# GpSimd takes the last eight rows of the small systems, and the solving of group 6, L1 and the last outputs are issued elsewhere

## The chip, the cores and the metric

The kernel runs on one core of a Trainium2 chip, as one launch of one program. Its engines are TensorE (PE in the profile, with PEld for its weight loads), VectorE (DVE), ScalarE (ACT), GpSimd (POOL) and SyncE (SP, which here only issues transfers). The metric is the device time of the launch in microseconds (us), lower is better. Times are medians of several executions; the profile is of one execution more.

## The reference, cut to what matters

A stream x of 128 sequences with 32 tokens of 128 channels runs through four layers. Each layer adds three blocks to the stream: cross attention, attention, and a feed-forward block.

```python
x = x + L0_xattn(layernorm(x), ctx)     # cross attention over 257 context rows, 16 heads
x = x + L0_attn(layernorm(x))           # kernel attention with landmarks, below
x = x + L0_ffn(layernorm(x))            # 8 experts, the best 2 of each token
x = x + L1_xattn(layernorm(x), ctx, mask); x = x + L1_attn(layernorm(x)); x = x + L1_ffn(layernorm(x))
...                                     # L2 and L3, three blocks each
```

The block around which the change turns is L0's attention. It solves one linear system for each sequence and head:

```python
Phi_Q = exp(-sq_dists(Q, landmarks) / temperature)
Phi_K = exp(-sq_dists(K, landmarks) / temperature)
W_kernel = exp(-sq_dists(landmarks, landmarks) / temperature) + REG * eye(64)
Z = einsum('bhnk,bhnd->bhkd', Phi_K, V)
Y = linalg.solve(W_kernel, Z)
out = einsum('bhnk,bhkd->bhnd', Phi_Q, Y)
norm = einsum('bhnk,bhko->bhno', Phi_Q, linalg.solve(W_kernel, sum(Phi_K, -2)[..., None]))
return (out / maximum(norm, 1e-10)) @ Wo.T + bo
```

L1's three blocks are a depooling cross attention, a state-space block (a convolution over time, a scan, a gate) and 16 experts of which each token uses 4.

## The kernel before, in words

**Groups.** The 4096 tokens are held in SBUF as eight groups (0 to 7) of 512 tokens, tiles `X0` to `X7` of 128 partitions x 4 x 128. A group is 16 sequences.

**Stage 1, L0's cross attention (`L0_xattn`).** A loop over 128 sequences, n = 0 to 127 (and two more turns to drain), 16 for each group. Each turn computes scores (line 544), reductions of their maximum on VectorE (546), exponentials on ScalarE (548), transposes and values on TensorE (566, 569, 583, 584). At the end of each turn `side_steps(3, 8)` advances other work, held in queues of Python generators: three steps of `kq` (the kernels of L0's attention, `L0_attn_kernels`, for the group before), steps of `sq` (the solving, `L0_attn_solve`) until the costs that they yield add up to 8, and one step of `oq` (the outputs, `L0_attn_out`). When the kernels of a group are through they append its solving to `sq`, and the solving appends its outputs to `oq`. So group 6's kernels run in the turns after n = 113, group 6's solving from about n = 120, and group 7's kernels begin when the loop is over.

**The solving (`L0_attn_solve`).** One group has 16 sequences x 16 heads = 256 systems of 32 unknowns (the 64 landmarks are folded onto the 32 tokens) with 9 right-hand sides. 128 partitions hold 2 systems each in a tile `A` of 32 rows x 2 x 41. It is loaded by 32 transfers, 16 of which read what the kernels stored (706) and 16 the right-hand sides (708). The elimination has 32 pivots k: a clamped reciprocal (712, 713), the scaled `row` (716), and then, for each block of eight rows below the pivot, a product into a temporary (722) and a subtraction from `A` (724), all on VectorE; ScalarE copies the row back (726). The matrix is symmetric, so the factors are read from row k itself. The back substitution has 31 products and subtractions (729, 731). The result goes to memory in eight transfers (737), and the outputs load it again for each tile of four sequences (748), multiply it with the other kernel matrix (756) and add the projection to `X` (770).

**Stage 2, L0's experts (`L0_ffn`).** Four chunks, m = 0 to 3, of two groups each. `L0_ffn_front` normalizes, routes, and sorts tokens by expert (`dispatch`, whose compares on VectorE fill tiles `dSL` for TensorE); `L0_ffn_blocks` runs 23 blocks of 128 gathered tokens through one expert's weights each, with gathers of tokens and weights issued by GpSimd; `L0_ffn_back` gathers the results in 16 gathers into tiles `G` and adds them to the stream (1026). TensorE's instructions of this stage stay in the order in which the program issues them: `order()` chains each to the one before. The fronts of chunks 0, 1 and 2 lie beside the kernels of group 7, chunk 0 and chunk 1. Chunk 3 holds groups 6 and 7, so its front needs their outputs.

Between blocks `side(nk, us, no, nl)` advances the queues of stage 1 (with a budget `us` for the solving and `no` steps of the outputs) and `nl` steps of `dq`, which from chunk 1's fourth block on holds L1 for groups 0 and 1, one generator of 28 steps each (2 of cross attention, 6 of the state-space block, 20 of the experts, 16 of which are one expert each). What is left of L1 at the end runs behind chunk 3.

**The rest.** `middle` runs L1 for groups 2 to 7 beside L2's cross attention and attention, then come L2's experts and L3. The change does not touch them. A scheduler places each engine's instructions when the program is built, within the dependencies and the chains above: an engine's queue need not be in the order of the source.

Of the kernel before, what the change touches and what calls it, by code (L numbers as in the profile page):

```python
# [9 lines left out]
FP = mybir.dt.float32  # L10
# [3 lines left out]
ALU = mybir.AluOpType  # L14
# [154 lines left out]
class Kern:  # L169
# [202 lines left out]
    def L0_xattn(self, W):  # L372
        nc = self.nc
        with self.pool("xw") as xw:
# [62 lines left out]
            with self.pool("xc") as xc, self.pool("xs", 2) as xs, \  # L437
# [5 lines left out]
                for n in range(B + 2):  # L443
# [29 lines left out]
                    if i == 3 and b == 1 and g + 1 < NG:  # L473
                        nxt = self.L0_xattn_group(g + 1, WNf, xc)
                    if t:
                        self.side_steps(3, 8)

    def follow(self, st, *insts):

# [213 lines left out]
    def L0_attn_solve(self, g):  # L693
# [16 lines left out]
        for k in range(T):  # L710
            p = sv.tile([128, HC], FP, tag="p", bufs=2)
            nc.vector.tensor_scalar(p, A[:, k, :, k], 1e-6, None, ALU.max)
            nc.vector.reciprocal(p, p)
            n = N - 1 - k
            row = sv.tile([128, HC, N], FP, tag="row", bufs=2)
            nc.vector.tensor_tensor(row[:, :, k + 1:N], A[:, k, :, k + 1:N], p.unsqueeze(2).to_broadcast([128, HC, n]), ALU.mult)
            yield 0.3 + 0.00107 * HC * n
            for i0 in range((k + 1) // RB * RB, T, RB):
                i0, i1 = max(i0, k + 1), i0 + RB
                m, n = i1 - i0, N - i0  # L720
                t = sv.tile([128, RB * HC * N], FP, tag="t", name="elt")[:, :m * HC * n].rearrange("p (i h j) -> p i h j", i=m, h=HC)
                nc.vector.tensor_tensor(t, A[:, k, :, i0:i1].rearrange("p h i -> p i h").unsqueeze(3).to_broadcast([128, m, HC, n]),  # L722
                                        row[:, :, i0:N].unsqueeze(1).to_broadcast([128, m, HC, n]), ALU.mult)
                nc.vector.tensor_tensor(A[:, i0:i1, :, i0:N], A[:, i0:i1, :, i0:N], t, ALU.subtract)  # L724
                yield 0.12 + 0.00214 * m * HC * n
            nc.scalar.copy(A[:, k, :, k + 1:N], row[:, :, k + 1:N])
        for k in range(T - 1, 0, -1):
            t = sv.tile([128, RB * HC * N], FP, tag="t", name="elt")[:, :k * HC * R].rearrange("p (i h j) -> p i h j", i=k, h=HC)
# [48 lines left out]
    def dispatch(self, pool, psum, tag, I8, n, k, E, NB):  # L777
# [63 lines left out]
        yield 1  # L841
        ps = psum.tile([128, NB], FP, tag=tag, name="pinv")
        for i in range(n * k):
            SL = pool.tile([128, 128], FP, tag="dSL", bufs=3)
            nc.vector.tensor_scalar(SL, self.j128, qf[:, i, 0:1], None, ALU.is_equal)
            nc.tensor.matmul(ps, lhsT=SL, rhs=BK[:, i, :], start=i == 0, stop=i == n * k - 1)
            if i % 4 == 3 and i < n * k - 1:
                yield 1
# [8 lines left out]
    def L0_ffn(self, w, W):  # L857
        nc = self.nc
        with self.pool("fs", 2) as fs, self.pool("fr", 2) as fr, \
# [25 lines left out]
            for m, c in enumerate(chunks):  # L885
# [1 line left out]
                if m + 1 < 4 and m < 2:  # L887
                    fr_ = self.L0_ffn_front(m + 1, chunks[m + 1], w, fs, fr, fpb, new)
                for b, _ in enumerate(self.L0_ffn_blocks(cur[0], fs, fpa, fpb)):
                    side(0, 4.0, int(m > 0 and (m < 2 or b > 18)))  # L890
                    if old and b == 3:
                        self.L0_ffn_back(*old, fs)
                        if m == 1:
                            self.dq = [self.L1(g, W) for g in range(2)]
                    if fr_ and b >= 3 and next(fr_, None) is None:
                        fr_ = None
                    order()
                while fr_ and next(fr_, None) is not None:
                    order()
                if m == 2:  # L900
                    while not self.ready.issuperset(chunks[3]):
                        side(1, 6.5, 1)
                        order()
                    for _ in self.L0_ffn_front(3, chunks[3], w, fs, fr, fpb, new):
                        side(0, 0, 0)
                        order()
# [112 lines left out]
    def L0_ffn_back(self, m, c, slot, rows, inv, E2, fs):  # L1019
        nc = self.nc  # L1020
        for i in range(8):
            x = self.X[c[i // 4]][:, i % 4, :]
            for j in range(2):
                G = fs.tile([128, 128], FP, tag="G", bufs=6)
                self.gather(G, self.ysd[m], slot[:, i, j:j + 1])
                nc.vector.scalar_tensor_tensor(x, G, E2[:, i, j:j + 1], x, ALU.mult, ALU.add)

# [907 lines left out]
```

## Time and profile before

| what | us |
|---|---|
| median of 3 runs | 5004.54 |
| lowest and highest run | 5003.34, 5005.09 |
| the profiled execution | 5007.62 |
| its span, first to last instruction | 5005.9 |
| end of L0's cross attention on TensorE | 2113.9 |
| last store of a kernel matrix of group 7 | 2203.4 |
| loads of group 7's systems, first and last issue | 2205.5, 2249.9 |
| solve 6: first pivot, end of back substitution | 2044.0, 2237.9 |
| solve 7: first pivot, end of back substitution | 2274.2, 2423.1 |
| chunk 0, first block and last | 2217.7, 2290.2 |
| chunk 1, first block and last | 2297.0, 2576.0 |
| chunk 2, first block and last | 2583.7, 2716.5 |
| chunk 3, first block and last | 2785.4, 2836.7 |
| last addition of chunk 3 | 2867.5 |

The span runs from the first to the last instruction of the profiled execution; its own time has 1.7 us more. Rows of the profile name a line of the kernel, an engine, an operation and the tiles, output first; a tile's buffer number is left out. A wait is put down to the instruction that released it.

### The profile page before, as it was taken

The page shows a single profiled execution, that of the slowest core. Times are in us where ns is not written, and L with a number is a line of the kernel's source. Part 1 is how long each engine was busy: PE and PEld are TensorE (multiplying, and loading weights), DVE is VectorE, ACT ScalarE, POOL GpSimd, SP SyncE. Part 2 cuts the span into 40 slices and gives each one's busy share as a digit, 9 for nine tenths or more (in the row PEclk, how much of TensorE's full clock was granted, in tenths as well). Part 3 has the DMA queues.
Part 4 walks back from the last instruction along what each step waited for, and adds up shares of the span by engine and source line. Part 5 has one row for each costly group of instructions (what it writes and reads, how often), then busy time and mean ns, then how long its engine had stood idle before and what let it go on. Part 6 is the DMA issues. An engine that isn't in the chain of part 4 may idle for free. (4 is left out here: it accounts for less than half of the span.)

```text
span 5005.9 us, 90275 instructions
## 1 busy us (share of the span) xinstructions
PE 4248.2 (85%) x33802; PEld 3111.7 (62%) x33802; DVE 3387.4 (68%) x10311; ACT 2347.2 (47%) x6637; POOL 1295.6 (26%) x1309
## 2 busy tenths in 40 slices
PE   7999999999898999875377798898898886879788
PEld 5777676767676776665365565666566653546455
DVE  5336758494948576777655478888898775777444
ACT  4555445454444444432233354545554554763333
POOL 1020211111110202035143513332332332322443
PEclk8999899999999998967677898999999987989677
DMA  4223131314141222255132410111011101000100
GB/s 139 61 60 57 39 66 42 66 39 72 38 72 35 56 53 56 49 121 144 37 107 86 138 35 23 31 29 28 27 29 32 37 20 46 1 1 16 32 14 10
DMA packets 388968, 255.95 MB, mean 51 GB/s; under 512 B 184545, under 2 KB 356961, under 8 KB 388017
## 3 DMA queue, kind: packets, MB, share of 16 engines
q1 hardware_dynamic: 361842, 191.22, 16.1%
q0 software_dynamic: 18240, 58.66, 4.0%
q8 instruction: 266, 4.36, 0.4%
q10 hardware_dynamic: 8448, 0.30, 0.2%
q14 instruction: 172, 1.41, 0.1%
HBM read 211.02 MB, written 39.08 MB: 50 GB/s over the span
## 5 line engine op out<-in xcount | busy, mean ns | idle before, releaser
L218 POOL TENSOR_TENSOR rs<-ve,w_const 128x4 f32<-128x4 f32 (+1 forms) x192 | 189.9, 990 | 1552.1 <-DVE ve L216 1278.4
L544 PE MATMUL S<-cT,q 128*128 128x257 f32 x2048 | 545.5, 407 | 18.5 <-ACT E L548 17.8
L544 PEld LDWEIGHTS S<-cT,q 128*128 128x128 f32 x2048 | 391.0, 201 | 145.7 <-issue 54.6
L546 DVE TENSOR_REDUCE nm<-S 128x1 f32<-128x257 f32 x512 | 214.8, 420 | 335.9 <-PE S L544 334.6
L1389 PE MATMUL S<-cT,QM 128*128 128x289 f32 x1024 | 326.4, 435 | 78.5 <-ACT E L1391 70.5
L548 ACT ACTIVATE E<-S,nm 128x257 f32<-128x257 f32 x512 | 242.3, 474 | 299.8 <-DVE nm L547 298.8
L1391 ACT ACTIVATE E<-S,nm 128x289 f32<-128x289 f32 x512 | 253.4, 499 | 194.8 <-DVE nm L1390 190.9
L722 DVE TENSOR_TENSOR elt<-A,row 128x400 f32<-128x400 f32 (+22 forms) x608 | 290.0, 477 | 6.4
L724 DVE TENSOR_TENSOR A<-A,elt 128x400 f32<-128x400 f32 (+22 forms) x608 | 291.2, 479 | 4.2
L527 PE MATMUL pq<-xT,WQK 128*128 128x128 f32 x2048 | 268.0, 290 | 14.1 <-ACT q L528 14.1
L1389 PEld LDWEIGHTS S<-cT,QM 128*128 128x128 f32 x1024 | 177.5, 198 | 161.8 <-ACT E L1391 72.3
L583 PE MATMUL po<-TA,cN 128*128 128x512 f32 x512 | 271.1, 612 | 4.7 <-DVE xn L224 3.9
L527 PEld LDWEIGHTS pq<-xT,WQK 128*128 128x128 f32 x2048 | 252.5, 200 | 24.7 <-ACT q L528 17.6
L584 PE MATMUL po<-TB,cN 128*128 128x512 f32 x512 | 265.5, 600 | 0.0
L558 ACT ACTIVATE E<-E,sm 128x256 f32<-128x256 f32 x512 | 220.2, 498 | 79.8 <-DVE sm L554 74.9
L241 POOL TENSOR_TENSOR QM<-QT,w_const 128x512 f32<-128x512 f32 x128 | 142.6, 1119 | 434.0 <-PE S L1389 410.7
L1390 DVE TENSOR_REDUCE nm<-S 128x1 f32<-128x289 f32 x512 | 219.8, 449 | 31.1 <-PE S L1389 28.3
L1400 PE MATMUL pt<-w_const,E 128*96 128x128 f32 (+1 forms) x1536 | 234.9, 290 | 0.0
L597 PE MATMUL pout<-WVO,OT 128*128 128x128 f32 x2048 | 234.2, 276 | 0.3 <-ACT OT L585 0.3
L597 PEld LDWEIGHTS pout<-WVO,OT 128*128 128x128 f32 x2048 | 231.7, 192 | 0.9 <-ACT OT L585 0.5
L1400 PEld LDWEIGHTS pt<-w_const,E 128*96 128x96 f32 (+1 forms) x1536 | 181.5, 145 | 61.6 <-issue 37.3
L1721 ACT ACTIVATE E<-S,nm 128x128 f32<-128x128 f32 x512 | 179.9, 397 | 64.6 <-DVE nm L1718 64.6
(526 smaller groups left out, 10357.3 us busy)
## 6 DMA issues: line engine op xcount, KB each, us to landing
cT<-ctxT SPq DMA_DIRECT2D x128, 257.0 KB
cN<-ctx SPq DMA_DIRECT2D x128, 256.0 KB
cT<-ctxT SPq DMA_DIRECT2D x32, 514.0 KB
phik<-PW SPq DMA_DIRECT2D x32, 256.0 KB
phiq<-P SPq DMA_DIRECT2D x32, 256.0 KB
A<-phik SPq DMA_DIRECT2D x128, 64.0 KB
PQ<-phiq SPq DMA_DIRECT2D x32, 256.0 KB
cN<-ctx SPq DMA_DIRECT2D x32, 194.0 KB
```

Source lines behind the costliest of these rows:

```text
L527: self.follow(st, nc.tensor.matmul(ps[:, k, :, :], lhsT=WQK[:, 4 * j + k, cb * 128:(cb + 1) * 128], rhs=t["x"], start=True, stop=True))
L544: self.follow(st, nc.tensor.matmul(S, lhsT=t["QP"][j][:, cb, b, :, :], rhs=t["cT"][b][:, cb, :], start=cb == 0, stop=cb == 1))
L548: nc.scalar.activation(E[:, j, 0:LK], S, AF.Exp, bias=m, accum_out=sm[:, j:j + 1])
L558: nc.scalar.activation(E[:, j, 0:256], E[:, j, 0:256], AF.Copy, scale=sm[:, j:j + 1])
L583: self.follow(st, nc.tensor.matmul(po, lhsT=cN[:, 0, c], rhs=TA, start=True, stop=False), nc.tensor.matmul(po, lhsT=cN[:, 1, c], rhs=TB, s ...
L584: nc.tensor.matmul(po, lhsT=cN[:, 1, c], rhs=TB, start=False, stop=True))
L597: self.follow(st, nc.tensor.matmul(po[:, 0, :], lhsT=OT[:, cb, h, :, :], rhs=WVO[:, cb, h, :], start=h == 0 and cb == 0, stop=False))
L722: nc.vector.tensor_tensor(t, A[:, k, :, i0:i1].rearrange("p h i -> p i h").unsqueeze(3).to_broadcast([128, m, HC, n]), row[:, :, i0:N].uns ...
L724: nc.vector.tensor_tensor(A[:, i0:i1, :, i0:N], A[:, i0:i1, :, i0:N], t, ALU.subtract)
L1389: self.follow(st, nc.tensor.matmul(S, lhsT=t["QM"][:, 0, 4 * j:4 * j + 4, :], rhs=t["cT"][:, b, :], start=True, stop=True))
L1391: nc.scalar.activation(E[:, j, :], S, AF.Exp, bias=nm[:, j:j + 1], accum_out=sm[:, j, b:b + 1])
L1400: self.follow(st, nc.tensor.transpose(pt[0:n, j * 128:(j + 1) * 128], E[:, j, k0:k1], self.ident))
```

## The change

Edits in the order of work, one of engine, and sizes of buffers:

- the turns of stage 1 from n = 120 on have a budget of 0 for the solving;
- in `L0_attn_solve`, for all groups but the last, the product and the subtraction for rows 24 to 31 are issued on GpSimd, with a temporary of their own (`tp`); such an update yields 0.01 in place of its cost; `row` has three buffers in place of two;
- in `L0_ffn` the budget of each block is 3.0 in place of 4.0; outputs are stepped only in chunk 1; L1 is stepped in every second block from chunk 1 on;
- behind chunk 2, L1 and the solving are stepped together until no solving is left and L1 of group 0 is through, then six steps of L1 alone, then the outputs, one for one with steps of L1, until chunk 3's groups are complete;
- `dSL` has two buffers in place of three, `G` three in place of six.

```diff
@@ L0_xattn
-                        self.side_steps(3, 8)
+                        self.side_steps(3, 8 if n < 120 else 0)
@@ L0_attn_solve
-            row = sv.tile([128, HC, N], FP, tag="row", bufs=2)
+            row = sv.tile([128, HC, N], FP, tag="row", bufs=3)
...
-                nc.vector.tensor_tensor(t, A[:, k, :, i0:i1].rearrange("p h i -> p i h").unsqueeze(3).to_broadcast([128, m, HC, n]),
-                                        row[:, :, i0:N].unsqueeze(1).to_broadcast([128, m, HC, n]), ALU.mult)
-                nc.vector.tensor_tensor(A[:, i0:i1, :, i0:N], A[:, i0:i1, :, i0:N], t, ALU.subtract)
-                yield 0.12 + 0.00214 * m * HC * n
+                eng = nc.vector
+                if g < NG - 1 and i0 == T - RB:
+                    eng = nc.gpsimd
+                    t = sv.tile([128, RB * HC * (RB + R)], FP, tag="tp", name="eltp").rearrange("p (i h j) -> p i h j", i=m, h=HC)
+                eng.tensor_tensor(t, A[:, k, :, i0:i1].rearrange("p h i -> p i h").unsqueeze(3).to_broadcast([128, m, HC, n]),
+                                  row[:, :, i0:N].unsqueeze(1).to_broadcast([128, m, HC, n]), ALU.mult)
+                eng.tensor_tensor(A[:, i0:i1, :, i0:N], A[:, i0:i1, :, i0:N], t, ALU.subtract)
+                yield 0.12 + 0.00214 * m * HC * n if eng is nc.vector else 0.01
@@ dispatch
-            SL = pool.tile([128, 128], FP, tag="dSL", bufs=3)
+            SL = pool.tile([128, 128], FP, tag="dSL", bufs=2)
@@ L0_ffn
-                    side(0, 4.0, int(m > 0 and (m < 2 or b > 18)))
+                    side(0, 3.0, int(m == 1), int(m < 1 or b % 2))
...
                 if m == 2:
+                    while self.sq or len(self.dq) > 1:
+                        side(0, 4.0, 0)
+                        order()
+                    for _ in range(6):
+                        side(0, 0, 0)
+                        order()
                     while not self.ready.issuperset(chunks[3]):
-                        side(1, 6.5, 1)
+                        side(0, 0, 1)
                         order()
@@ L0_ffn_back
-                G = fs.tile([128, 128], FP, tag="G", bufs=6)
+                G = fs.tile([128, 128], FP, tag="G", bufs=3)
```

## The prediction

> **What bounds the kernel now.** I read the page's sums, then the stages, then the waits of TensorE in the stage with most idle time, then single rows.
>
> The page says that no engine is full:
>
> ```profile
> span 5005.9 us, 90275 instructions
> ...
> PE 4248.2 (85%) x33802; PEld 3111.7 (62%) x33802; DVE 3387.4 (68%) x10311; ACT 2347.2 (47%) x6637; POOL 1295.6 (26%) x1309
> ```
>
> So I cut the span at events: the end of the cross attention (2114), of the last kernels (2204), solve 7 from its first pivot to its last back substitution (2274 to 2423), the first block of expert chunk 2 (2584), its last (2717), the first of chunk 3 (2785), its last (2840). Columns are the stretch, its length, and the busy time of each engine.
>
> ```profile
> core 0: us, PE busy (x) PEld busy (x) DVE busy (x) ACT busy (x) POOL busy (x), PEclk, DMA share, GB/s
> 1876.00:2114.00 238.00, 218.65 (x1940) 162.81 (x1939) 157.95 (x510) 115.62 (x306) 40.57 (x43) 0.93 0.22 46
> ...
> 2274.00:2423.00 149.00, 52.02 (x387) 47.45 (x387) 123.34 (x389) 29.40 (x100) 55.91 (x49) 0.63 0.28 85
> ...
> 2584.00:2717.00 133.00, 91.44 (x540) 73.70 (x540) 58.64 (x173) 52.06 (x126) 57.17 (x58) 0.82 0.36 102
> 2717.00:2785.00 68.00, 53.16 (x262) 39.63 (x260) 52.47 (x179) 13.70 (x26) 31.62 (x32) 0.77 0.21 65
> 2785.00:2840.00 55.00, 50.92 (x417) 46.44 (x419) 10.75 (x25) 37.93 (x112) 32.54 (x34) 1.00 0.68 215
> 2840.00:2876.00 36.00, 9.26 (x39) 5.59 (x32) 19.69 (x53) 6.50 (x8) 20.91 (x21) 0.58 0.30 88
> ```
>
> Cross attention is TensorE's (92% in the first row). Solve 7 is VectorE's, with TensorE at 35%. The waits of TensorE between 2340 and 2460 name the hole:
>
> ```profile
> engine line waited for: us in total, times, longest us
> PE ko L756 <- DVE Yb L690: 76.1, 1, 76.1
> ```
>
> TensorE's queue is in program order in this layer; the outputs of group 7 (L756) stand between blocks 5 and 6 of chunk 1, and need solve 7. From there 17 blocks, all of L1 for groups 0 and 1, and chunks 2 and 3 follow in 430 us.
>
> **The rows on GpSimd.** For groups 0 to 6 the updates of rows 24 to 31 move: 24 pivots x 2 instructions x 7 groups = 336. On VectorE they are these rows:
>
> ```profile
> L724 DVE TENSOR_TENSOR A<-A,elt 128x272 f32<-128x272 f32 x192 | 84.0, 437 | 0.2
> L722 DVE TENSOR_TENSOR elt<-A,row 128x272 f32<-128x272 f32 x192 | 83.2, 433 | 1.5
> ```
>
> 0.87 us a pivot, 20.9 a solve leave VectorE. GpSimd has no such row; with two dense inputs L606 takes 0.452 at 128 elements and L671 1.265 at 512, so 0.75 at 272 for the subtraction; with a broadcast operand L949 takes 0.40 at 128 and L241 1.05 at 512, so 0.64 for the product. 1.39 a pivot, 33 us a solve, and GpSimd has room (41 of 238 us busy in the first row). But both engines then read SBUF with two inputs each, which the trace shows to collide. VectorE, then GpSimd, in the same 4 us:
>
> ```profile
> 845.34 0.55 DVE L731 TENSOR_TENSOR A<-A,elt 128x378 f32<-128x378 f32 x1
> 845.93 1.48 DVE L729 TENSOR_TENSOR elt<-A 128x360 f32<-128x360 f32 x1
> 847.44 1.48 DVE L731 TENSOR_TENSOR A<-A,elt 128x360 f32<-128x360 f32 x1
> ```
>
> ```profile
> 845.70 1.32 POOL L671 TENSOR_TENSOR PW<-P,DDt 128x512 f32<-128x512 f32 x1 [1.41 <-issue]
> 847.09 1.43 POOL L672 TENSOR_TENSOR PW<-PW,eyt 128x512 f32<-128x512 f32 x1
> ```
>
> An undisturbed 128x360 takes 0.53; each loses 0.95 to a GpSimd operation of 1.27 (undisturbed). A small one, L604 of 0.454 us, stretched a VectorE row of 0.15 to 0.41 at 753.7, by 0.27. Between these points: 0.42 for the product, 0.52 for the subtraction, 0.94 a pivot if each meets a two-input VectorE operation. Of VectorE's durations while solve 4 runs in the changed program's order (50.1 of solving in 66.8 us) 75% are such, so 0.70: against 0.87 removed, VectorE gains 0.17 a pivot, 4 us a solve. The Trainium skill ("SBUF — State Buffer", Who interferes with whom) says that the loser blocks for the full instruction: 1.39 x 0.75 = 1.04, a loss of 0.17 a pivot, 4 us a solve the other way, and 13 us if all of it is met. I take the rows, because they have the pipelined ends in them; the bounds for one solve are -8 (no collision, and 40% of the 20.9 felt by TensorE, which is 92% busy anyway) to +12 (24 x 0.52).
>
> How that reaches TensorE: the steps of a solve are paced by the costs that it yields, 8 per iteration, and a moved update yields 0.01. A solve falls from 93 to 77, so its elimination takes some 6 iterations in place of 7, each denser. While solving, an iteration took 15.4 us (seven between 696 and 804) against 12.2 in group 0 (sixteen between 93 and 288, no solving); denser ones cost about what fewer ones save. Six solves, 0 to 5: -10, bounds -48 and +72. Behind the moved operations GpSimd queues the norm's `pow` (L218), needed only at the next group; ScalarE's copy of the row (L726) waits for GpSimd's product, which can start as soon as the row is there, so no later than VectorE's last one did. A new wait stands at pivot 24, whose row is GpSimd's: the score reductions queue behind it on VectorE, and TensorE's transposes wait for those. `row` has three buffers, so GpSimd is at most three pivots late, 3 x 1.39: 0 to 4 us a solve, in the bounds.
>
> **Group 6's solving.** Nothing is stepped from n = 120 on. The order in which the built program holds its instructions still lets part of it rise there: 19 us of durations before the last score reduction, 46 before the change. The last iterations get some 9 us shorter. Then VectorE's queue holds, up to the end of solve 7, 348 us of durations (counts by line and shape times medians of the profile) where it held 296, which took 310. But solve 7 starts with its loads: they wait for the last kernel's store (2203), are issued until 2250, and the first pivot follows at 2274. Solve 6 now fills that hole instead of running before; its longer instructions delay the kernels' steps, so I give back 7 of the 9: pivot at 2272. From there to the last back substitution the queue holds 190 us in place of 142 (L1 of group 0, 16; the dispatch and norms of chunk 2, some 27; outputs, 11, and others). 142 took 149; short instructions overlap, and 48 more at 0.85 make 190: solve 7 ends at about 2465, 42 later. SP's stores, loads and the two group 7 tiles that the order leaves ahead of chunk 2 took 36 us before (2423 to 2459): chunk 2 starts at about 2503, 81 us earlier than at 2584, since its 17 blocks, chunk 2's dispatch and the start of L1 now lie beside the solve. On GpSimd 14 of solve 6's operations (10 us) stand ahead of gathers of chunk 0; its blocks (2218 to 2290) need not end before the outputs of group 6, so that is hidden; uncovered, it is 10.
>
> **L1 and the last outputs.** Chunk 2 carries 11 experts' steps of L1 in place of 24 steps. Thirteen blocks with 13 steps took 62 us (2584 to 2645), 4.8 a pair; a block alone 2.3 (23 in 52, chunk 3). So 11 x 4.8 + 12 x 2.3 = 80, say 82, against 133: -51. What it no longer carries is then exposed: L1 of group 1 starts when that of group 0 is through. 7 expert steps at 3 (2712 to 2727 for 5): 20; from the last one to the first matmul of L1's cross attention 12 and from that to the router 57, as in group 1 before; the front of chunk 3 behind it 55 to 60 (its logits at 2729, block 0 at 2785). 20 + 12 + 57 + 7 + 56 = 152, against 68: +84. The last two outputs (12 each) lie beside that chain. Chunk 3 carries 6 expert steps, 6 x 2.5: +15. Behind it TensorE waits for L1 of group 2 (2840 to 2876 above, 9 of 36 busy); that starts later in relation to the blocks, since L1's buffers come free later: +8. Sum of the layer: -81 - 51 + 84 + 15 + 8 = -25.
>
> **Buffers.** G from 6 to 3: a gather every 1.25 us, landed after 2.6, added in 0.35 and released: 3.3 for three, under 3 x 1.25, so nothing while VectorE is prompt; up to 6 in the last back. dSL from 3 to 2: a compare waits for a matmul two back; 0 to 5 in the one exposed front. I take 0 for both.
>
> **Sum.** -25 - 10 = -35 on an execution whose span is 5005.9, 5007.6 in all, 3 above the median of the runs, 5004.5: 4970.
>
> **Rivals.** (1) The whole hole is won: the chain of L1 for group 1 overlaps chunk 2 (VectorE is at 59 of 133 us there, so nothing but buffers holds it back) and group 2's L1 doesn't lag: -60 for the +84, -8: about 4900. Against it: L1's tiles have one buffer. (2) Nothing remains: the end of solve 7 comes 25 us later than I say (each extra VectorE us between 2272 and its end counts fully), 4995 to 5014. (3) Slower: the collision. Each of the 144 pivots in the cross attention costs 1.39 - 0.87 = 0.52 if GpSimd holds VectorE for its whole duration, and reductions (L546) that TensorE needs stand behind the held instruction: 75 us, less 25: 5055. It decides from 25/144 = 0.17 a pivot. For it: 0.95 us losses in the rows above; against it: 25% of VectorE's time is PSUM reads that weren't stretched (L546 beside L604: 0.41).
>
> **Numbers.** Forecast 0.40 (-70 to -10, the likeliest one's own range 4935 to 4995), rival 1 0.20, rival 2 0.10, rival 3 0.30. Faster by over 0.2% (10 us, about what a measurement here can tell) 0.60, within 0.10, slower 0.30. 8 in 10: half of rival 1 and most of 3, 4905 to 5035.
>
> **What would show it.** Right: the 76.1 us wait of L756 gone; solve 7 ending near 2465, 42 us behind the old one, chunk 2 starting near 2500, chunk 3 near 2735; an iteration while solving within 1 us of 15.4; VectorE's 128x400 rows stretched by about 0.5 beside GpSimd. Wrong: groups of the cross attention over 275 us (268 now), or chunk 3 starting after 2780.

## The result

The changed kernel takes 5079.67 us (median of 3 runs, 5079.12 to 5089.88) against 5004.54 before: a ratio of 1.0157, 95% interval 1.0134 to 1.018. It is 75 us slower where 4970 was forecast. The engines' sums on the page of the changed kernel show no cause:

```profile
span 5087.9 us, 90607 instructions
...
PE 4262.5 (84%) x33802; PEld 3105.1 (61%) x33802; DVE 3394.6 (67%) x9975; ACT 2342.5 (46%) x6630; POOL 1579.3 (31%) x1645
```

VectorE has 336 instructions less and is as busy as before (3387.4 then); GpSimd is 284 us busier. The stages tell where the time went. They are the six stretches shown of before, cut at the same events: group 7 of the cross attention, solve 7, chunk 2, the gap to chunk 3, chunk 3, the tail. Columns are the stretch, its length, the busy time of each engine with its instructions, the granted clock of TensorE, the DMA share and GB/s.

```profile
core 0: us, PE busy (x) PEld busy (x) DVE busy (x) ACT busy (x) POOL busy (x), PEclk, DMA share, GB/s
1986.00:2222.00 236.00, 213.98 (x1941) 158.50 (x1940) 133.82 (x399) 113.07 (x291) 53.51 (x57) 0.95 0.22 47
2390.00:2606.00 216.00, 129.89 (x812) 114.13 (x811) 158.59 (x545) 69.82 (x196) 96.88 (x94) 0.71 0.42 118
2635.00:2716.00 81.00, 71.44 (x502) 63.63 (x503) 34.03 (x96) 41.06 (x118) 45.30 (x47) 0.90 0.54 159
2716.00:2864.00 148.00, 92.97 (x406) 62.72 (x406) 96.91 (x322) 24.61 (x40) 43.64 (x44) 0.64 0.11 33
2864.00:2924.00 60.00, 57.32 (x465) 53.06 (x465) 17.56 (x50) 37.64 (x113) 31.95 (x34) 1.00 0.66 197
2924.00:2960.00 36.00, 13.10 (x32) 3.76 (x31) 23.96 (x53) 9.87 (x12) 23.67 (x21) 0.55 0.23 62
```

| marks, us | before | forecast | after |
|---|---|---|---|
| period of a group of the cross attention, groups 3 to 6 | 267 to 270 | about 266 | 283 to 287 |
| end of the cross attention | 2113.9 | 2095 | 2221.8 |
| from there to the first pivot of solve 7 | 160 | 167 | 168 |
| to its last back substitution | 309 | 360 | 384 |
| to the first block of chunk 2 | 470 | 398 | 414 |
| length of chunk 2, then the gap to chunk 3 | 133, 69 | 82, 152 | 76, 153 |
| to the last addition of chunk 3 | 753.6 | 738 | 729.6 |
| from the last addition to the end of the span | 2138.4 | the same | 2136.5 |

The end of 2095 takes off both the 10 us of the six solves and the 9 of the last turns. The prediction's marks behind it leave the 10 out, so they are counted here from 2105.

The whole loss is in the cross attention: +107.9 there, -24.0 in the layer of experts, -1.9 behind it, together +82.0, the difference of the two spans (5087.9 less 5005.9). The row of group 7 has VectorE at 133.8 of 236 us where 158.0 of 238 stood before: it has less to do (a part of solve 6 has left these turns, and the rows have), but TensorE still needs 286 us for a group. From the end of group 0 (288 us) to that of the cross attention, before and then after:

```profile
288.00:2114.00 1826.00, 1685.23 (x14661) 1283.05 (x14660) 1223.27 (x4139) 900.55 (x2417) 280.67 (x302) 0.94 0.26 52
```

```profile
288.00:2221.00 1933.00, 1696.87 (x14662) 1277.66 (x14661) 1222.29 (x3779) 901.65 (x2412) 537.32 (x605) 0.94 0.24 49
```

TensorE waits 236 us in place of 141 (the stretch less its busy time), at the same granted clock. The rows of TensorE's score matmul on the page, before and then after, say what it waits for (busy time, mean ns, idle time just before it and its releaser):

```profile
L544 PE MATMUL S<-cT,q 128*128 128x257 f32 x2048 | 545.5, 407 | 18.5 <-ACT E L548 17.8
```

```profile
L544 PE MATMUL S<-cT,q 128*128 128x257 f32 x2048 | 549.8, 407 | 98.7 <-ACT E L548 98.4
```

80 us of new waits for the exponentials of an earlier score. ScalarE makes those from maxima that VectorE reduces. In the experts the forecast wait (76.1 us for L756, now L760) has shrunk; the waits of TensorE from 2400 to 2640:

```profile
engine line waited for: us in total, times, longest us
...
PE ko L760 <- issue: 22.7, 1, 22.7
...
PE ko L760 <- DVE Yb L690: 7.6, 1, 7.6
```

The 22.7 us is what is left of it: it ends at 2619.5, after solve 7 (2606) and the load of its result, though the profile names no releaser. The 7.6 us ends at 2419.9 and stands before group 6's outputs.

GpSimd's new rows are the subtraction, estimated at 0.75 us, and the product, estimated at 0.64:

```profile
L728 POOL TENSOR_TENSOR A<-A,eltp 128x272 f32<-128x272 f32 x168 | 143.6, 855 | 12.9
...
L726 POOL TENSOR_TENSOR eltp<-A,row 128x272 f32<-128x272 f32 x168 | 135.6, 807 | 433.9 <-DVE row L716 355.4 <-DVE TL L555 38.5 <-DVE nm L547 21.2
```

### The profile page after: what moved, and what is told of

Read it like the earlier page. It is cut to its first block, busy times and chain, and to the rows that moved or that the text cites. A ratio compares the mean times of both kernels' runs of the same rounds, so it can differ in the third digit from the quotient of the medians.

```text
span 5087.9 us, 90607 instructions
## 1 busy us (share of the span) xinstructions
PE 4262.5 (84%) x33802; PEld 3105.1 (61%) x33802; DVE 3394.6 (67%) x9975; ACT 2342.5 (46%) x6630; POOL 1579.3 (31%) x1645
## 5 line engine op out<-in xcount | busy, mean ns | idle before, releaser
L546 DVE TENSOR_REDUCE nm<-S 128x1 f32<-128x257 f32 x512 | 214.6, 419 | 389.1 <-PE S L544 388.2
L726 POOL TENSOR_TENSOR eltp<-A,row 128x272 f32<-128x272 f32 x168 | 135.6, 807 | 433.9 <-DVE row L716 355.4
L726 DVE TENSOR_TENSOR elt<-A,row 128x400 f32<-128x400 f32 (+28 forms) x440 | 240.8, 547 | 24.6 <-DMA yd<-Yt 18.5
L728 DVE TENSOR_TENSOR A<-A,elt 128x400 f32<-128x400 f32 (+28 forms) x440 | 247.6, 563 | 4.3
L585 ACT COPY OT<-po 128x512 f32<-128x512 f32 x256 | 149.1, 582 | 159.7 <-PE po L584 158.1
```

The lines of the kernel that those rows point to most:

```text
L726: eng.tensor_tensor(t, A[:, k, :, i0:i1].rearrange("p h i -> p i h").unsqueeze(3).to_broadcast([128, m, HC, n]), row[:, :, i0:N].unsqueeze ...
L728: eng.tensor_tensor(A[:, i0:i1, :, i0:N], A[:, i0:i1, :, i0:N], t, ALU.subtract)
```

## Which part does it

Below, marks of the cross attention are compared between runs directly, since its group 0, in which nothing is solved, lasts 195.1 to 196.2 us in every kernel looked at. Whole times are compared by the ratio to the kernel before measured beside each: it took 4996 us beside the first four kernels and 5045 to 5050 beside the others, so an absolute number in an expectation has to be read against that. Lengths in the layer of experts are not compared between these two sets: e13 below takes as long as the kernel before beside it (1.0000) with some 798 us in that layer, where the trace of before has 753.6.

**All edits of order, rows on VectorE, and the reverse.**

```diff
  e1_rows_vector, against the change
-                if g < NG - 1 and i0 == T - RB:
+                if False:
  e2_rows_gpsimd_alone: the kernel before, with the rows on GpSimd and the three sizes of buffers
```

> The whole change, but all rows of the elimination stay on VectorE with their full costs. If the rows on GpSimd (by collision or by pacing) cost the 108 us that cross attention grew by, its end comes back to 2100 to 2115 us and the time falls to 4960 to 4985, below the kernel before, since the experts' layer gained about 25. If the order of the layer's work or the solving withheld from n = 120 costs the time, it stays above 5040.

> The kernel before, with the rows on GpSimd (yielding 0.01) and the three buffer sizes, and none of the edits of order. If the rows cost the time, cross attention ends at 2200 to 2225 and the time is 5090 to 5120, above the whole change, because the experts' layer gains nothing. If not, 4995 to 5010.

The first gives 0.9924 (0.9899 to 0.995), 4960.6 us; its cross attention ends at 2109.2, its layer lasts 715.7 us in place of 753.6. The second gives 1.0276 (1.0241 to 1.0311), and its cross attention ends at 2223.6, as in the change. So the order edits gain 38 us and nearly all of it in the experts; the rows on GpSimd cost 117 beside them (1.0157 less 0.9924, times 5004.5).

**Is it the pacing?** A moved update yields 0.01, so that a turn takes more steps.

```diff
  e3_rows_gpsimd_paced, against the change
-                yield 0.12 + 0.00214 * m * HC * n if eng is nc.vector else 0.01
+                yield 0.12 + 0.00214 * m * HC * n
  e4_rows_vector_dense: rows on VectorE as in e1, and these updates yield 0.01
```

> The whole change, rows on GpSimd, but such an update yields its full cost, so an iteration gets as much of the solving as before. Pacing theory (the 0.01 packs 77 in place of 93 units, more pivots per turn): cross attention comes back to within 30 us of 2114, the time to 4970 to 5010. Collision theory (GpSimd's reads hold VectorE and the score path wherever they stand): the end stays above 2180, the time above 5045.

> The whole change with the rows on VectorE, but yielding 0.01: the pacing of the change without GpSimd. Pacing theory: as slow as the change or slower, cross attention ending at 2210 or later, since VectorE has 21 us more of work in the same turns. Collision theory: near the version with rows on VectorE and full costs, the end below 2150.

1.0087 (1.0055 to 1.0118), end of the cross attention at 2189.2, and 0.9912 (0.9878 to 0.9946), at 2089.5. The yields alone do no harm with the rows on VectorE. With the rows on GpSimd the full yields bring back 0.007 of 0.023, and the loss stays.

## What the rows on GpSimd do

Four readings of the loss were open: VectorE's instructions are stretched beside GpSimd's; ScalarE's copy of the row, in front of the exponentials in ScalarE's queue, waits for GpSimd's product; the late pivots have become a chain through GpSimd; the program is laid out in a worse order.

**Without GpSimd's instructions, and with instructions that nothing waits for.**

```diff
  e5_rows_left_out, against the change
-                eng.tensor_tensor(t, A[:, k, :, i0:i1].rearrange("p h i -> p i h").unsqueeze(3).to_broadcast([128, m, HC, n]),
-                                  row[:, :, i0:N].unsqueeze(1).to_broadcast([128, m, HC, n]), ALU.mult)
-                eng.tensor_tensor(A[:, i0:i1, :, i0:N], A[:, i0:i1, :, i0:N], t, ALU.subtract)
+                if eng is nc.vector:
+                    eng.tensor_tensor(t, A[:, k, :, i0:i1].rearrange("p h i -> p i h").unsqueeze(3).to_broadcast([128, m, HC, n]),
+                                      row[:, :, i0:N].unsqueeze(1).to_broadcast([128, m, HC, n]), ALU.mult)
+                    eng.tensor_tensor(A[:, i0:i1, :, i0:N], A[:, i0:i1, :, i0:N], t, ALU.subtract)
  e9_gpsimd_beside, against the change
-                eng.tensor_tensor(t, A[:, k, :, i0:i1].rearrange("p h i -> p i h").unsqueeze(3).to_broadcast([128, m, HC, n]),
+                eng.tensor_tensor(t, (A[:, k] if eng is nc.vector else row)[:, :, i0:i1].rearrange("p h i -> p i h").unsqueeze(3).to_broadcast([128, m, HC, n]),
...
-                eng.tensor_tensor(A[:, i0:i1, :, i0:N], A[:, i0:i1, :, i0:N], t, ALU.subtract)
+                if eng is nc.vector:
+                    eng.tensor_tensor(A[:, i0:i1, :, i0:N], A[:, i0:i1, :, i0:N], t, ALU.subtract)
+                else:
+                    eng.tensor_tensor(t, t, t, ALU.subtract)
```

> The changed kernel without the 336 instructions on GpSimd: the updates of rows 24 to 31 are left out for groups 0 to 6 (that part of the solve is not computed), the steps are given out as in the change. It is the floor for the work itself: VectorE has 125 us of rows less in the cross attention than with the rows on VectorE (4957 with the same pacing). All theories expect it below 4957; if TensorE feels a fifth of the 125, about 4935, cross attention ending near 2070. If it came out above 5000, the cost would lie in the order in which the program is laid out, not in GpSimd's instructions.

> As the run with the rows left out, but GpSimd carries out two instructions of the same shape at the same places, which read the pivot's row and write a scratch tile: nothing waits for them but the buffers of the row. It shows collision without dependence (rows 24 to 31 are again not updated). Collision theory: what GpSimd takes from VectorE's access costs the time, so within 25 us of the change, 5055 or more, cross attention ending after 2195. Queue theory (ScalarE's copy of the row waits for GpSimd's product and holds the exponentials behind it) and late-pivot theory (the pivots from 16 on are a chain through GpSimd): at most 30 above the run with the rows left out, so about 4965, cross attention ending near 2095.

Left out: 0.9863 (0.9845 to 0.9881), the cross attention ends at 2093.2. With instructions beside: 1.0095 (1.0074 to 1.0116), at 2195.5. The order is not to blame, since it is the same in the two: all 9975 instructions of VectorE stand in the same order. Nor are waits for GpSimd's results, of which there are none. What remains is what GpSimd's running does to the other engines' instructions. The stretching of VectorE's can be seen one instruction at a time. Pivot 18 of solve 3 on VectorE without GpSimd (start, length, instruction):

```profile
1308.76 0.17 DVE L712 TENSOR_SCALAR p<-A 128x2 f32<-128x2 f32 x1
1308.97 0.17 DVE L713 RECIPROCAL p<-p 128x2 f32<-128x2 f32 x1
1309.24 0.20 DVE L716 TENSOR_TENSOR row<-A,p 128x44 f32<-128x44 f32 x1
1309.48 0.39 DVE L726 TENSOR_TENSOR elt<-A,row 128x220 f32<-128x220 f32 x1
1309.90 0.39 DVE L728 TENSOR_TENSOR A<-A,elt 128x220 f32<-128x220 f32 x1
1310.32 0.17 DVE L712 TENSOR_SCALAR p<-A 128x2 f32<-128x2 f32 x1
```

The same instructions with GpSimd beside them, and then GpSimd at that time:

```profile
1368.00 0.49 DVE L712 TENSOR_SCALAR p<-A 128x2 f32<-128x2 f32 x1
1368.52 0.17 DVE L713 RECIPROCAL p<-p 128x2 f32<-128x2 f32 x1
1368.82 0.20 DVE L716 TENSOR_TENSOR row<-A,p 128x44 f32<-128x44 f32 x1
1369.06 0.39 DVE L726 TENSOR_TENSOR elt<-A,row 128x220 f32<-128x220 f32 x1
1369.48 0.73 DVE L729 TENSOR_TENSOR A<-A,elt 128x220 f32<-128x220 f32 x1
1370.25 0.49 DVE L712 TENSOR_SCALAR p<-A 128x2 f32<-128x2 f32 x1
```

```profile
1367.74 0.72 POOL L731 TENSOR_TENSOR eltp<-eltp 128x272 f32<-128x272 f32 x1
1369.17 0.80 POOL L726 TENSOR_TENSOR eltp<-row 128x272 f32<-128x272 f32 x1 [0.71 <-DVE row L716]
1370.05 0.67 POOL L731 TENSOR_TENSOR eltp<-eltp 128x272 f32<-128x272 f32 x1
```

The clamp of the pivot (L712), two elements a partition, takes 0.49 in place of 0.17: it starts at 1368.00 and ends at 1368.49, 0.03 after GpSimd's subtraction that began before it (1367.74 + 0.72). The next one does the same (1370.74 and 1370.72). The subtraction at 1369.48, begun under GpSimd's product, takes 0.73 in place of 0.39; the product at 1369.06, begun 0.11 ahead of GpSimd's, keeps its 0.39. From pivot to pivot 2.25 us pass in place of 1.56.

Summed over all instructions of six solves, one by one against the run without, VectorE is stretched by 14.3 us a solve, 86 in all: 0.60 a pivot of the 24. 4.9 of a solve's 14.3 fall on two small ones, the clamp (1.9) and the minimum behind each score reduction (L547, 128x1; 3.0). The cross attention pays 102 us for these 86. (The sums of stretching move by up to 4 us with where a solve is taken to begin and end.) TensorE's busy time and its waits, from 288 us to its end, without and then with GpSimd beside:

```profile
288.00:2093.00 1805.00, 1650.22 (x14659) 1249.77 (x14658) 1107.75 (x3782) 898.67 (x2411) 283.79 (x302) 0.96 0.25 53
```

```profile
PE S L544 <- ACT E L548: 49.0, 49, 2.4
...
PE pq L527 <- ACT q L528: 11.6, 13, 1.1
...
PE ptl L591 <- ACT TA L572: 7.3, 14, 0.9
```

```profile
288.00:2195.00 1907.00, 1686.97 (x14655) 1271.01 (x14656) 1198.42 (x3774) 900.99 (x2411) 514.21 (x602) 0.95 0.24 50
```

```profile
PE S L544 <- ACT E L548: 88.6, 46, 4.8
...
PE pq L527 <- ACT q L528: 25.1, 19, 1.9
PE ptl L591 <- ACT TA L572: 19.5, 14, 3.6
```

TensorE waits 40 us longer for exponentials, 13 for queries, 12 for copies on ScalarE (whose own busy time is the same, 899 and 901); and its own matmuls, the same ones, are busy 37 us longer, at a granted clock of 0.95 where it was 0.96. Before rounding the trace's means are 0.946 and 0.964, and 1650 x 0.964 / 0.946 is 31 us more. So of the 102, 65 are waits and some 31 go with the clock; why the clock is lower is not shown.

The same row for e1, which has the rows on VectorE:

```profile
288.00:2109.00 1821.00, 1685.55 (x14663) 1284.91 (x14662) 1204.35 (x4070) 900.43 (x2411) 281.51 (x303) 0.94 0.27 52
```

From here to the run with the rows left out VectorE is rid of 97 us of busy time, and yet TensorE waits 155 us in place of 135 (the yields differ too; e4 is taken in below). The 16 us by which that run ends earlier come with TensorE being busy 35 us less, at the higher clock, not with shorter waits.

**ScalarE's queue, and the late pivots.**

```diff
  e7_row_copy_later, against the change
-            row = sv.tile([128, HC, N], FP, tag="row", bufs=3)
+            row = sv.tile([128, HC, N], FP, tag="row", bufs=4)
...
-            nc.scalar.copy(A[:, k, :, k + 1:N], row[:, :, k + 1:N])
+            late.append((k, row))
+            if len(late) > 1 or k == T - 1:
+                for j, r in late[:1] if k < T - 1 else late:
+                    nc.scalar.copy(A[:, j, :, j + 1:N], r[:, :, j + 1:N])
+                del late[:1]
  e8_rows_gpsimd_k16
-                if g < NG - 1 and i0 == T - RB:
+                if g < NG - 1 and i0 == T - RB and k < 16:
```

> The change with ScalarE's copy of a pivot's row issued one pivot later (behind the updates of the next pivot), with four buffers for the row in place of three. Queue theory: TensorE's wait for the exponentials (98 us for S in the change, 18 before) falls to under 40, and half or more of the 119 us that the rows on GpSimd cost come back: 5020 or less. Collision and late-pivot theories: nothing changes, 5070 to 5085, and the wait for the exponentials stays above 80.

> The change with the rows on GpSimd for pivots 0 to 15 only: 32 of the 48 instructions of a solve, and from pivot 16 on the rows are VectorE's. Late-pivot theory: most of the 119 us are gone, 4985 or less, cross attention ending before 2130. Collision and queue theories: the cost goes with the count, 16 of 24, so about 4960 + 79 = 5040, cross attention ending near 2185.

The first: 1.0127 (1.0107 to 1.0146), not told apart from the change's 1.0157 by the intervals; the cross attention ends at 2217.4, 4 us earlier. Its page row of the score matmul still has 99.5 us of waits for the exponentials. In the seven last turns of a group the copies wait as they did, in the change and then here:

```profile
ACT A L730 <- POOL eltp L726: 7.4, 7, 2.2
```

```profile
ACT A L734 <- POOL eltp L727: 8.8, 8, 2.2
```

GpSimd is simply as late one pivot further on. So this run did not take the wait away and does not test the queue. The run with instructions beside does: there the copies wait for nothing of GpSimd's, and most of the loss stands. The queue can have a part only in the 26 us between its end and that of the change. The second: 0.9959 (0.9939 to 0.9979), cross attention to 2149.5. The ratio is what the late-pivot reading asked for (4984 of 5004.5); the end of the cross attention lies between the two. Its complement tells:

```diff
  e10_rows_gpsimd_late
+                if g < NG - 1 and i0 == T - RB and k >= 16:
  e14_gpsimd_one_input, against e9_gpsimd_beside
+                    eng.tensor_scalar(t, row[:, :, i0:N].unsqueeze(1).to_broadcast([128, m, HC, n]), 1.5, None, ALU.mult)
-                    eng.tensor_tensor(t, t, t, ALU.subtract)
+                    eng.tensor_scalar(t, t, 1.5, None, ALU.subtract)
```

> The complement of the run with pivots 0 to 15: the rows on GpSimd for pivots 16 to 23 only, 16 of the 48 instructions of a solve. Ratios to the kernel before: rows on VectorE 0.992, all on GpSimd 1.016, pivots 0 to 15 on GpSimd 0.996. Late pivots special (short pivots, in which GpSimd's two instructions leave VectorE no free time): the missing 0.020 lies here, ratio 1.010 or more. Collision by count, with a part of it hidden as long as VectorE has room left in the iteration: eight pivots alone find that room too, ratio at most 1.000, and the dear ones are those that come on top.

> As the run with instructions on GpSimd beside the solve that nothing waits for (ratio 1.0095; without them 0.9863; rows 24 to 31 are not updated in either), but each of the two has one input and a constant in place of two inputs, with the same output of 272 elements. If it is the reading of two inputs by both engines that makes VectorE stand: VectorE's instructions keep the lengths they have without GpSimd, ratio at most 0.990, cross attention ending near 2085. If any GpSimd instruction costs VectorE as much: 1.005 or more, ending near 2190.

The late pivots alone give 0.9883 (0.985 to 0.9917), the cross attention ends at 2115.1: no cost that could be seen, and the late-pivot reading falls. The one-input instructions give 0.9965 (0.9954 to 0.9975), end at 2140.5, between both expectations. They are longer than those with two inputs,

```profile
L731 POOL TENSOR_SCALAR eltp<-row 128x272 f32<-128x272 f32 x168 | 172.3, 1025 | 306.6 <-DVE row L716 243.7 <-DVE TL L555 38.5 <-DVE sm L553 10.1
...
L732 POOL TENSOR_SCALAR eltp<-eltp 128x272 f32<-128x272 f32 x168 | 168.2, 1001 | 13.6
```

(801 and 730 ns with two inputs), but stretch VectorE by 5.2 us a solve, not 14.3. So it is mostly not the mere presence of GpSimd; whether the second input makes the difference, or the operation that changed with it, these two runs do not part.

**Why do the parts not add up?** 16 pivots cost 0.004 over rows on VectorE, 8 late ones nothing, all 24 cost 0.023. Two explanations were tried. The first: the collision is dear only in turns that are full; a budget of 3 puts the elimination two turns later, into the long turns of the kernels.

```diff
  e15_gpsimd_three (rows on GpSimd) and e16_vector_three (rows on VectorE)
-                        self.side_steps(3, 8 if n < 120 else 0)
+                        self.side_steps(3, 3 if n < 120 else 0)
```

> The change, rows on GpSimd at all pivots, with a budget of 3 in place of 8 for the solving in each turn. In VectorE's queue the elimination then begins and ends about two turns later: its last pivots stand in turns that carry a fresh group's kernels, which last 23 to 30 us for TensorE's sake. Overfull-turn theory (the collision costs time only where VectorE's turn has no room left): the rows on GpSimd cost half or less of what they did, ratio at most 1.005, period of the groups at most 276 us. Every-collision theory (each us that VectorE's instructions are stretched is paid): nothing changes, 1.012 or more, period 284 or more.

> The pair to the run before: all edits of order, rows on VectorE, a budget of 3 for the solving. Both theories expect about what a budget of 8 gave, 0.988 to 0.996, period of the groups 263 to 269 us; above 1.000 the later solving would itself cost, and the pair would have to be read by its difference alone.

In this pair the solving falls so far behind in the source that chunk 2 is routed before groups 4 and 5 have their attention, so the values are others and the work is the same. 1.0095 (1.006 to 1.0129) and 0.9885 (0.9852 to 0.9918), ends at 2156.7 and 2053.6. The first ratio lies between its two expectations; read as a pair, the rows on GpSimd cost 0.021 and 103 us at this place too, against 0.023 and 112. The periods of groups 3 to 6, 270 to 282 us and 275 on average, would by themselves have spoken for the full turns (at most 276), but in the pair's other half they are 254 to 266. The theory of the full turns falls. The second splits the collision at a fixed order, and puts it on the order of e1, which holds 24 pivots in the last seven turns of a group where the change holds 32:

```diff
  e17_beside_early and e18_beside_late, against e9_gpsimd_beside
+                if eng is nc.vector or k < 16:
...
-                else:
+                elif k < 16:
  e18_beside_late: the same with k >= 16
  e19_vector_and_beside, against e1_rows_vector
+                if g < NG - 1 and i0 == T - RB and k < 24:
+                    u = sv.tile([128, RB * HC * (RB + R)], FP, tag="tp", name="eltp").rearrange("p (i h j) -> p i h j", i=RB, h=HC)[:, :m, :, :n]
+                    nc.gpsimd.tensor_tensor(u, row[:, :, i0:i1].rearrange("p h i -> p i h").unsqueeze(3).to_broadcast([128, m, HC, n]),
+                                            row[:, :, i0:N].unsqueeze(1).to_broadcast([128, m, HC, n]), ALU.mult)
+                    nc.gpsimd.tensor_tensor(u, u, u, ALU.subtract)
```

> The run with two-input instructions on GpSimd that nothing waits for, kept for pivots 0 to 15 only (rows 24 to 31 not updated, VectorE's order the same in all of this family). Without any: 0.9863; with all 24: 1.0095, 0.0232 more, 86 us of stretching of which two thirds belong to these pivots. Sum of the stretching: two thirds of it, 1.001 to 1.004. Slack that takes the first part free: at most 0.996.

> The same for pivots 16 to 23 only. Sum of the stretching: a third of 0.0232, so 0.993 to 0.996. Slack that takes the first part free: at most 0.989, and the two parts together fall short of the whole by 0.008 or more. If both lie where the sum has them, the order in which VectorE's instructions were built, spread over more turns in the kernels with a part of the rows on GpSimd, is what made those parts cheap.

> All edits of order, rows on VectorE (ratio 0.992), and beside them GpSimd carries out the two instructions a pivot that nothing waits for, at all 24 pivots. VectorE keeps the spread order of that kernel, 24 pivots in the last seven turns of a group in place of 32, and has all its rows and the stretching too. Order theory (the collision is cheap where the elimination is spread): the addition costs under half of 0.0232, ratio at most 1.003. Sum of the stretching: 1.013 or more.

| kernel | ratio (interval) | stretching of VectorE, six solves | end of the cross attention, against |
|---|---|---|---|
| e18, 8 late pivots | 0.9954 (0.9933 to 0.9974) | 28 us | 2128.5, +35 to e5 |
| e14, one input, 24 pivots | 0.9965 (0.9954 to 0.9975) | 31 us | 2140.5, +47 to e5 |
| e17, 16 early pivots | 0.9991 (0.9979 to 1.0004) | 52 us | 2148.8, +56 to e5 |
| e9, 24 pivots | 1.0095 (1.0074 to 1.0116) | 86 us | 2195.5, +102 to e5 |
| e19, 24 pivots, rows on VectorE too | 1.0089 (1.0061 to 1.0116) | 86 us | 2201.3, +92 to e1 |

The stretching is each instruction's length less that of the same instruction in the run without (in e19 10,134 of 10,311 stand at the same place). At a fixed order it adds up: 0.0128 and 0.0091 for the two parts, 0.0232 for the whole; 0.9991 is a little under the 1.001 expected. The order of e1 pays for it too: 0.0165, between the two expectations and nearer the sum, and its cross attention ends 92 us later for 86 us of stretching. Each us by which VectorE's instructions are stretched costs about 1.1 to 1.5 us here; there is no free first part. In TensorE's waits alone (from 288 us on) it is +23 (e18), +24 (e14), +43 (e17), +65 (e9), all against e5, and +68 (e19, against e1): 0.75 to 0.83 us for each us of stretching. What comes on top, 12 to 37 us, is longer busy time at a lower granted clock.

So it is on the other side that the parts differ: what TensorE gets back for the rows that leave VectorE. With all 24 it is nearly nothing: e1 to e5 takes away 125 us of VectorE's rows in six solves and the cross attention ends 16 earlier; against e4 (2089.5), which has e5's yields, it ends 4 later, with 155 us of TensorE's waits in place of 129. With 8, collision (+35 by e18) and relief (42 us of rows gone) come to +6, but TensorE's waits are 155 us in e10 against 135 in e1, nearly the 23 of e18, so the relief is not in the waits there either. The built order of VectorE's queue would fit: of a solve's 32 pivots, the last seven turns of group 4 hold 24 in e1, 20 in e10, 29 in e8 and all 32 in e5 and the change, so that the room which the rows leave is filled with pivots that had stood in later turns. But no run here changed that packing alone: why the relief nearly makes up for the collision with 8 pivots and not with 24 stays open.

**The edits of order.**

```diff
  e13_vector_g6_before, against e1_rows_vector
-                        self.side_steps(3, 8 if n < 120 else 0)
+                        self.side_steps(3, 8)
  e6_rows_gpsimd_g6, against the change
-                if g < NG - 1 and i0 == T - RB:
+                if g == NG - 2 and i0 == T - RB:
```

> All edits of order, rows on VectorE, but the steps from n = 120 on keep their budget of 8 for the solving, as before the change. By the forecast the edit shortens the end of the cross attention by 9 and gives 7 back in the layer: so within 10 us of the run with all edits of order (ratio 0.992), 0.990 to 0.996, with the last values some 5 to 9 us later. If the starting of solve 6 behind the kernels is what moves chunk 2 forward, 1.000 or more.

> All edits of order, the rows on GpSimd for group 6 alone, whose solve lies behind the cross attention, where VectorE and not TensorE sets the end. By the measured collision VectorE loses 0.60 a pivot and is rid of 0.87: 6 us gained at the start of solve 7, ratio 0.991 against 0.992 with all rows on VectorE. If the collision costs more there than it removes (the layer of the change lasts 730 us, with the rows on VectorE 716): ratio 0.994 to 0.996.

The first: 1.0000 (0.9988 to 1.0011). The whole gain is gone, with the wait back at its old length (waits of TensorE from 2200 to 2800):

```profile
PE ko L760 <- DVE Yb L690: 76.2, 1, 76.2
```

Solve 7 ends earlier, 63 us before that of e1 (2461.0 against 2523.9), but group 7's outputs stand inside chunk 1 again: their loads are issued at 2472 to 2492, behind solve 7, and TensorE waits for them between blocks 7 and 8. In e1 these loads come at 2541 to 2552 and 2627 to 2637, and all of chunk 1 (2280 to 2469) and the first ten blocks of chunk 2 lie beside solve 7. The other edits need that one to gain anything. The second: 0.9908 (0.9875 to 0.9941), not told apart from e1; inconclusive.

## Why the prediction was wrong

**The failed step** is "How that reaches TensorE": "denser ones cost about what fewer ones save. Six solves, 0 to 5: -10, bounds -48 and +72". Measured against the same kernel with its rows on VectorE it is +112 (2221.8 less 2109.2). The price a pivot was netted on VectorE, 0.87 removed less 0.70 of collision, as if TensorE felt both alike. It doesn't. By the chain of runs: the removed rows give back 16 us of 125 (2109.2 to 2093.2, e1 to e5), and with e5's yields nothing (2089.5, e4); GpSimd's instructions cost 102 for 86 of stretching (2195.5, e9); and the change has 26 more (2221.8), with 20 us more of stretching in it and the waits for GpSimd's results. In ratios: 0.9924, 0.9863, 1.0095, 1.0157. The upper bound of +72 failed for the same reason: it priced the worst collision, 1.39, but still took off 0.87.

**The sizes of the collision were good.** Forecast 0.94 if always met, 0.70 with a share of 75%; measured 0.60 with nothing waiting, and some 0.74 in the change (17.7 us a solve, where 9,235 of 9,975 instructions stand at the same place as in e9). The rule of the Trainium skill ("SBUF — State Buffer", Who interferes with whom), taken as the full length of GpSimd's instructions times 75%, gave 1.04, or 1.25 with the lengths they turned out to have; the trace of e9 shows that the clamp, when it begins under one of GpSimd's two-input instructions, is indeed held to its end (30 of 30, last section), but VectorE's instructions begin part way, so that less is lost; under one-input ones (e14) most clamps are not held so long, against the rule. In lengths of instructions VectorE did gain the few us a solve that the step said. In busy time it did not: lengths overlap, and e5 is less busy than e1 by 117.5 us in seven solves (3270.9 against 3388.4), 0.70 a pivot and not 0.87; the change is busier than e1 by 6 us (3394.6).

**An iteration while solving** was to stay within 1 us of 15.4. The last seven turns of group 4 take 122 us in the change, 17.4 each, and 106, 15.1, before. The threshold of 275 us a group, named as what would make it wrong, was passed at 283 to 287.

**ScalarE's copy of the row** does wait for GpSimd's product (7.4 us in seven turns, above), against the step's "no later than VectorE's last one did", but issuing it later bought 4 us. **Pivot 24**: VectorE waits for GpSimd's subtraction 17.0 us in seven solves, 2.4 a solve, inside the 0 to 4 forecast.

**The layer of experts: -16, measured -24.0.** The -25 of the prediction counts from the start of the span and holds the 9 us of the last turns of the cross attention; from the end of those it is -16, and that -25 looks like -24.0 is luck. The terms, from there: chunk 2 starts 56 us earlier, where 72 was forecast (solve 7 takes 216 us from its first pivot, forecast 190); chunk 2 57 shorter, forecast 51; the exposed chain +84, forecast +84; chunk 3 +5, forecast +15; the tail +1, forecast +8. With the rows on VectorE the layer gains 38. What the step did not see is that all of it hangs on the one edit from n = 120 on, to which it gave 9 less 7 us.

**Rival 3** had the direction and a part of the mechanism: work that TensorE needs stands on VectorE behind held instructions. Its price of 75 us, again 1.39 less 0.87, was a third too low: 5055 for 5080. Against it stood that reductions from PSUM aren't stretched; that is true (L546 takes 419 to 420 ns on average with and without GpSimd) and didn't help, since the minimum of one element behind each of them is. The row of 0.15 us that the prediction read as stretched to 0.41 was such a minimum; VectorE and then GpSimd, in the trace of before:

```profile
753.74 0.41 DVE L547 TENSOR_TENSOR nm<-nm,nsn 128x1 f32<-128x1 f32 x1
```

```profile
753.56 0.58 POOL L604 TENSOR_TENSOR xn<-xn,w_L_xln 128x128 f32<-128x128 f32 x1 [0.53 <-DVE xn L224]
```

It was used as a point between sizes, and not as a link of TensorE's chain.

## What to carry to other kernels

Work that is moved from VectorE to GpSimd isn't priced by the difference of two busy times: if VectorE's instructions stand in a chain that TensorE waits for, each us that GpSimd stretches them can cost TensorE a us or more (here 1.1 to 1.5, 0.8 of it in waits), while the removed work may be worth nothing to TensorE. The two can be measured apart by a kernel that leaves the rows out and one that runs GpSimd's instructions for nobody, in the same order. Here the better kernels keep the rows on VectorE: 0.9924 and 0.9912 (e1 and e4), or move only those of the last eight pivots, 0.9883, which the intervals do not tell apart.

## What the hardware did that was not expected

- A VectorE instruction of two elements a partition with one input (L712) was held as long as a large one: 0.17 to 0.49 us. Those that read PSUM (L546, 0.42; the copy L573 of 128x512, 0.69) kept their length beside GpSimd. So did the 54 reciprocals of two elements (L713) that began under a one-input operation of GpSimd in e14.
- GpSimd's two-input operations of 272 elements stretched VectorE nearly three times as much as one-input operations of the same size that last 28 to 37% longer (14.3 and 5.2 us a solve). Under the two-input product or subtraction in e9 all 30 clamps that would otherwise have ended before it ended with it, within 0.08 us; under the one-input operations in e14 only a quarter of 59 did.
- TensorE's waits were not all of what it lost: the same matmuls of the cross attention (14,659 and 14,655 recorded) were busy 1687.0 us in place of 1650.2 when it waited more. The granted clock, 0.946 for 0.964 on average, makes some 31 of these 37. It is lower over whole executions too: 0.887 to 0.893 in four of e9, 0.896 to 0.898 in four of e5. What lowers it is not shown.
